# A four-layer graph network on one core: layer 3's self-interaction made during layer 2, its edge factors made for 8 tiles at a time, record gathers by fours, and five single banks for layer 0's matrices

## The chip, the core and the metric

The kernel runs on one core of a Trainium2 chip. Its metric is the device time of one execution in microseconds (us); the median of several runs is compared. Five engines work in parallel, each with its own instruction stream: TensorE (PE in the profile, with its weight loads as PEld), VectorE (DVE), ScalarE (ACT), GpSimd (POOL) and SyncE (SP), which in this kernel issues most of the plain DMA transfers. POOL issues the indirect DMAs, that is, the gathers.

## The reference, cut to what matters

8192 nodes have 32 features each. 262144 edges are sorted by their target `dst`. Each of four layers adds its result to its input and normalizes the sum over the 32 features.

```python
x = layernorm(x + segment_sum(einsum('ei,eio->eo', x[src], W0[edge_type]), dst))   # layer 0, 64 matrices of 32x32
x = layernorm(x + segment_sum(x[src] * edge_weight[:, None], dst))                 # layer 1
x = layernorm(x + segment_sum(x[src], dst))                                        # layer 2
# layer 3: s = x[:, :8], v = x[:, 8:] as (8, 3); sh = edge_attr_4, f = edge_attr_32
h = relu(f @ W1 + b1);  w = (h @ W2 + b2).reshape(e, 4, 8, 8)                      # 64 hidden, 256 weights an edge
m0 = 0.25 * (s[src]*sh0 @ w[:, 0] + C110 * (v[src] . sh1) @ w[:, 3])
m1 = 0.25 * ((s[src] @ w[:, 1]) x sh1 + v[src]*sh0 @ w[:, 2])
out = segment_sum(concat(m0, m1), dst) + SI_SCALE * concat(s @ si_w0, v @ si_w1)   # the last term: self-interaction
x = layernorm(x + out)
```

## The kernel before

The program is written as one stream per engine, in an order set by hand. `V`, `A`, `PE`, `G` and `S` are the streams of DVE, ACT, TensorE, POOL and SP. `X.mark(ins)` lets an instruction raise its engine's semaphore, `X.after(mark)` makes the next instruction of stream X wait for a mark, and `now(X)` is the last mark of X so far. A `Landing` is the same for DMAs. All buffers are cut from one arena in SBUF by `Carve`, and the eight PSUM banks (128x512 f32 each) are called by number. An edge tile is 128 edges; there are 2048 of them.

**The table stage** writes `ytab`, the product of every node with each of the 64 matrices of layer 0, in 64 tiles of 1 MB: two pairs of matmuls (L404), an eviction of each pair (L410) and one store by SP (L412). Which engine evicts is decided by `busy`: while it is true, both pairs go to ACT, afterwards the second goes to DVE. Between the tiles runs a generator, `beginnings()`, one step a tile. It counts the edges of each node and then lets POOL gather 64 sets of records (source, target and weight of the edges, in order of the nodes; 98 KB each) with `indirect` (L383). All 64 are issued in one step. `busy` becomes false at the end of the generator. It also makes `row`, the row number of each edge in `ytab`.

**Layer 0** goes over 256 groups of 8 tiles. In each group DVE makes the one-hot matrix of the targets (`one_hot`, L505) and splits the gathered rows into three bf16 parts (`parts`, L619 to L624); PE sums them by target (L657) into bank 0 or 1, four groups to a bank. POOL gathers the rows of group g+12 from `ytab`: the first half of a group waits for the sums of group g, the second half for everything that PE was given in group g. From group 8 on, PE also makes the dense matrices of layers 1 and 2 out of the records, 256 times `matrices(i)` (L555 to L581), about one in each group. These are four units of eight matmuls (L571), each into a pair of banks, 3 and 4 or 5 and 6 in turn. ACT evicts a unit with two instructions of 128x512, one (L575) for `cmat` in bf16, one (L576) for `amat` in f32, and SP stores both (L580, L581). PE waits, ahead of a unit, for L576 of the unit before the last. The generator's records first pass `slots()` at group 4. When groups enough are done, `windows` (L495) and `normalize` (L454 and the lines after) make 8 x 128 nodes of the layer's output, through bank 2.

**Layers 1 and 2** are multiplications with these matrices, read back from HBM in 32 chunks of `amat` (L730) and 16 chunks of `cmat` (L733), with two buffers. ACT copies the sums of a chunk (L739), and `turn` (L710) transposes those of the chunk before and normalizes. `normalize` of layer 2 also writes `xtab`, the table of layer 3, through SP.

**Layer 3** begins with POOL's gathers from `xtab`, by quads of four tiles; 512 quads in all. `AHEAD` is 12: the gathers of quad q+12 wait for the W2 product of quad q. Beside the first gathers PE, ACT and DVE make the self-interaction, 16 steps of transpose (L852), copy (L854), matmul (L856) and addition (L858) into `z`. `factors(s)` (L825 to L836) makes, for 32 tiles at once and with DVE, the products of gathered features and `sh`; it waits until all 32 tiles have landed. It is called once ahead of the loop and then every eighth quad, for the next 32 tiles. A step of the loop makes the hidden layer for two quads (L883) with its relu on ACT (L891), the W2 product of one quad (L907) in one of two pairs of banks, five products on DVE (L944, L947, L951 three times), the one-hot of the quad (L505), and, four quads later, the sums by target on PE (L916). `windows` and `normalize` end it.

Of the kernel before, what the change touches and what calls it, by code (L numbers as in the profile page):

```python
# [16 lines left out]
OP = mybir.AluOpType  # L17
# [7 lines left out]
D = 32  # L25
# [120 lines left out]
def raw_layers(tc, x, a, w0, w1, b1, w2, si, m, bad):  # L146
# [136 lines left out]
    def beginnings():  # L283
# [71 lines left out]
        own(V, V.e.tensor_scalar(idx2, idx, RG - 1, None, op0=OP.bitwise_and))  # L355
        im = own(V, V.e.tensor_scalar(idx, idx, RG.bit_length() - 1, None, op0=OP.arith_shift_right))

        G.after(im)
        r_ld = Landing(tc, "ld_rec")
        for k in range(64):  # L360
            begun["rec"] = r_ld.add(indirect(rg[:, k].rearrange("p s f -> p (s f)"), a["rec"], idx[:, k:k + 1]))
        yield

        own(V, V.e.tensor_tensor(pre[:, f, :], idx2, deg, op=OP.add))
        own(V, V.e.tensor_reduce(ok[:, 3:4], pre[:, f, :], AX.X, OP.max))
        V.after(src_in, row_in)
        begun["row"] = own(V, V.e.scalar_tensor_tensor(row, src, float(R), row, op0=OP.mult, op1=OP.add))
        V.e.tensor_reduce(ok[:, 0:1], rel, AX.X, OP.max)
# [171 lines left out]


    oh_used = [None, None]
    bank_free = [None, None]
    st_ld = [Landing(tc, f"st_m{k}") for k in range(2)]
# [3 lines left out]
    def matrices(i):  # L548

        b, pp, k0 = i % 2, i // 2, 16 * (i % 2)  # L550
        WB = 8
        if i % WB == 0:
            n = min(WB * 16, CB * 16 - i * 16)
            V.after(now(V))
            own(V, V.e.tensor_copy(w_ps[:, 0:n], meta_w.rearrange("p n k -> p (n k)")[:, i * 16:i * 16 + n]))  # L555
        V.after(oh_used[b])
        own(V, V.e.tensor_tensor(oh_k[:, b, :, 0, :], iota[:, None, 0:64].to_broadcast([P, 16, 64]),  # L557
                                 meta_k[:, pp, k0:k0 + 16, None].to_broadcast([P, 16, 64]), op=OP.is_equal))
        V.e.tensor_tensor(oh_l[:, b], iota[:, None, :].to_broadcast([P, 16, P]),  # L559
                          meta_l[:, pp, k0:k0 + 16, None].to_broadcast([P, 16, P]), op=OP.is_equal)  # L560
        wo = (i % WB) * 16
        vm = V.mark(V.e.tensor_tensor(oh_k[:, b, :, 1, :], oh_k[:, b, :, 0, :],
                                      w_ps[:, wo:wo + 16, None].to_broadcast([P, 16, 64]), op=OP.mult))
        PE.after(vm)
        for q in range(4):
            bk = 3 + 2 * (units[0] % 2)
            PE.after(bank_free[units[0] % 2])
            for j in range(4):
                for h in range(2):
                    hs_ = slice(64 * h, 64 * h + 64)  # L570
                    ins = PE.e.matmul(bank[:, bk + h, :].rearrange("p (c s j) -> p c s j", s=64, j=4)[:, :, :, j],  # L571
                                      oh_l[hs_, b, 4 * q + j, :], oh_k[hs_, b, 4 * q + j], start=True, stop=True)
            pm = PE.mark(ins)
            A.after(pm, st_ld[b].mark() if q == 0 and st_ld[b].n else None)
            A.e.activation(st_c[:, b, q], bank[:, bk:bk + 2, 0:256], AF.Copy)  # L575
            bank_free[units[0] % 2] = am = A.mark(A.e.activation(st_a[:, b, q], bank[:, bk:bk + 2, 256:512], AF.Copy))  # L576
            units[0] += 1
        oh_used[b] = pm
        S.after(am)
        st_ld[b].add(S.e.dma_start(amat[:, 2048 * i:2048 * (i + 1)], st_a[:, b].rearrange("p u h c -> p (u h c)")))  # L580
        st_ld[b].add(S.e.dma_start(cmat[:, 2048 * i:2048 * (i + 1)], st_c[:, b].rearrange("p u h c -> p (u h c)")))  # L581
# [5 lines left out]
    agg_free = [freed[0], freed[0]]  # L587
    acc_free = [None]
    G.after(r0, *y_done)
# [49 lines left out]
    for g in range(GG + 2):  # L639
        if g >= 2 and (g - 2) % per == per - 1:  # L640
            vm = bank_out((g - 2) // per)
            while done < NB // LC and ready(done) <= g - 1:
                pm = windows(done, bank[:, 2, 0:LC * D], (acc_free[0], vm))
                acc_free[0] = normalize(0, done, bank[:, 2, 0:LC * D], pm, x_a, x_b)
                done += 1
# [26 lines left out]
    x3 = cut(NB, 3 * D, dt=BF)  # L672
    sums = cut(2, 512)
    end = (now(PE), now(V), now(A), *stored)
    S.after(*end)
# [23 lines left out]
    pend = None  # L699
    outs = [0]  # L700

    def turn(l, c, n, am):
# [15 lines left out]
    for n, (l, c) in enumerate(seq):  # L718
# [23 lines left out]
        if pend:  # L742
            turn(*pend)
        pend = (l, c, n, am)
    turn(*pend)


    cut = Carve()
    xg = cut(4, WT, D)
    win = cut(GG, D)  # L750
    free = [now(PE), now(V), now(A)]
    taken[:] = [[None] * (WT // TP) for _ in range(4)]
# [4 lines left out]
    hs = cut(4, 512)  # L757
    si_s, sis = cut(P), cut(P)
    z = cut(NB, D)
    zx = cut(2, P)  # L760
    ef = cut(3, 2, 512)
    sh = cut(3, WT, 4)
    a0 = cut(2, WT, 16)
    vs = cut(WT, 8, 3)
    a1 = cut(WT, 8)
    vm = cut(2, WT, 3, 8)
# [6 lines left out]
    oh = cut(NO, 4, P)  # L773
    r1 = cut(24)


# [5 lines left out]
    for h in range(2):  # L782
        c_ld.add(S.e.dma_start(b1_s[64 * h:64 * h + 64], b1))
    c_ld.add(S.e.dma_start(w2_s[0:65], w2))
    zm = V.mark(V.e.memset(si_s, 0.0))
    for k in range(4):
        hm = V.mark(V.e.memset(hs[64:65, k], 1.0))  # L787
    S.after(zm)
    for q in range(4):
        c_in = c_ld.add(S.e.dma_start(si_s[q * D:(q + 1) * D, q * D:(q + 1) * D], si))  # L790

# [15 lines left out]

    AHEAD = 12
    rows = {}

    def fetch_rows(q):

        if q < NQ:
            G.after(quad.get(q - AHEAD, {}).get("w"))
            rows[q // 8] = gathers(xtab, src, q // 8, q % 8 * 4, 4)

    def factors(s):

        k, landed = rows[s]
        b = batch[s]  # L820
        b["xg"] = k
        shv = sh[:, s % 3]
        u = s % 2
        V.after(b["s"])
        sm = V.mark(V.e.tensor_scalar(shv, shv, ALPHA, None, op0=OP.mult))  # L825
        V.after(*landed, sm)
        xv = xg[:, k]
        v = xv[:, :, 8:].rearrange("p t (i m) -> p t i m", m=3)
        vmk = V.mark(V.e.tensor_tensor(vs, v, shv[:, :, None, 1:4].to_broadcast([P, WT, 8, 3]), op=OP.mult))
        V.e.tensor_tensor(a0[:, u, :, 0:8], xv[:, :, 0:8], shv[:, :, 0:1].to_broadcast([P, WT, 8]), op=OP.mult)  # L830
        V.e.tensor_tensor(vm[:, u].rearrange("p t m i -> p t i m"), v,
                          shv[:, :, None, 0:1].to_broadcast([P, WT, 8, 3]), op=OP.mult)
        V.after(vmk)
        rm = V.mark(V.e.tensor_reduce(a1, vs, AX.X, OP.add))
        V.after(rm)
        b["f"] = V.mark(V.e.tensor_scalar(a0[:, u, :, 8:16], a1, float(C110), None, op0=OP.mult))  # L836


    V.after(c_in)
    V.after(V.mark(V.e.tensor_scalar(sis, si_s, float(SI), None, op0=OP.mult)))  # L840
    fetch(0)
# [3 lines left out]
    A.after(*free)  # L845
    sv = (V.sem, V.n)
    zf = [None, None]
    for j in range(NB // 4):
        xv = x_b[:, 4 * j:4 * j + 4, :].rearrange("p d f -> p (d f)")
        u = j % 2  # L850
        PE.after(zf[u])
        tm = PE.mark(PE.e.transpose(bank[:, 3 + u, 0:P], xv, ident))  # L852
        A.after(tm)
        am = A.mark(A.e.activation(zx[:, u], bank[:, 3 + u, 0:P], AF.Copy))  # L854
        PE.after(am, sv)
        pm = PE.mark(PE.e.matmul(bank[:, 5 + u, 0:P], zx[:, u], sis, start=True, stop=True))  # L856
        V.after(pm)
        zf[u] = zm = V.mark(V.e.tensor_add(z[:, 4 * j:4 * j + 4, :].rearrange("p d f -> p (d f)"),  # L858
                                           bank[:, 5 + u, 0:P], xv))
    PE.after(*zf)  # L860
    A.after(c_in, hm)

    h_free = zm
    w_free = [zm, zm]
    agg_free = [zm, zm]
    quad = {}
# [29 lines left out]
    factors(0)  # L896
    PE.after(c_in)
    hidden(0)
    for q in range(NQ + LAG3 + 2):
# [20 lines left out]
        prev = (V.sem, V.n)  # L920
        if q % 8 == 6 and q // 8 + 1 < NS:
            s = q // 8 + 1
            factors(s)
        V.after(prev)
        if q < NQ:
            V.after(batch[q // 8]["f"])
        V.after(quad.get(q - NP, {}).get("a"))
# [10 lines left out]
        if q < NQ:  # L938
            k, wp = quad[q]["k"]
            s, u = q // 8, (q // 8) % 2  # L940
            qs = slice((q % 8) * 4, (q % 8) * 4 + 4)
            pq = p[:, q % NP]
            V.after(quad[q]["w"])
            V.e.tensor_tensor(pr[:, q % 2].rearrange("p t (o i) -> p t o i", i=8),  # L944
# [5 lines left out]
            for mm in range(3):  # L950
                V.e.tensor_tensor(pq[:, :, 128 + 64 * mm:192 + 64 * mm].rearrange("p t (o i) -> p t o i", i=8),  # L951
                                  wp[:, :, 192:256].rearrange("p t (o i) -> p t o i", i=8),
                                  vm[:, u, qs, mm, None, :].to_broadcast([P, 4, 8, 8]), op=OP.mult)
            ins = one_hot(oh[:, q % NO], 4 * q, 4)
        if ins is not None:
# [500 lines left out]
```

## Time and profile before

| | us |
|---|---|
| median of 3 runs (7660.74, 7668.28, 7670.0) | 7668.28 |
| profiled execution, its own time | 7583.78 |
| its span in the profile | 7581.8 |
| first gather from `ytab` (start of layer 0's gathers) | 271.44 |
| last gather of layer 0 starts at about | 3433.5 |
| first gather from `xtab` | 4522.57 |
| first W2 product (L907) | 4595.0 |
| last gather ends | 7500.0 |
| last sum by target (L916) ends | 7560.95 |

The profile covers one execution, on the only core; its own time is 1.1% below the median of the runs. Two groups of instructions hold nearly all of POOL's time: 2048 gathers from `ytab` (1962.0 us, 958 ns each) and 2048 from `xtab` (1967.3 us, 961 ns each). PE's largest groups are the matrices' matmuls (L571, 1566.7 us, 365 ns each), the sums of layer 3 (L916, 1420.3 us) and the W2 products (L907, 1075.3 us). In the rows of the profile a line ends with the idle time ahead of an instruction and with what released it; "remote" stands for a releaser that the profile does not name, and "issue" for time in which the engine waited for nothing that it shows.

### The profile page before, as it was taken

To read this page: it belongs to the slowest core of one execution; us is meant where nothing else is said; L and a number is where in the kernel's file an instruction comes from. 1 tells how busy PE (TensorE), PEld (TensorE's weight loads), DVE (VectorE), ACT (ScalarE), POOL (GpSimd) and SP (SyncE) were. 2 spreads that over 40 slices of the span, in tenths; PEclk is the share of its full clock that TensorE was granted. 3 is DMA by queue.
4 is the path that set the end of the run, shared out by engine and by line. 5 is a ranking of instruction groups with operands and counts; after the bars stand their busy time and mean duration, and the time that the engine had idled before them with its cause. 6 is when DMAs were issued, how large, how long until landed. Compare 5 with 4: busy or idle time off the path is not lost.

```text
span 7581.8 us, 85791 instructions
## 1 busy us (share of the span) xinstructions
PE 5254.6 (69%) x34036; PEld 3717.5 (49%) x34036; DVE 4352.7 (57%) x8312; ACT 1629.6 (21%) x2812; POOL 3996.6 (53%) x4174
## 2 busy tenths in 40 slices
PE   5326665556555665654544867889989988888998
PEld 2115555555555555553222434555555555555555
DVE  3336676677676767764000005666666667666676
ACT  3213333333333333332000001111111111111111
POOL 3466565656566666650000016666666666666663
PEclk7557677777777777777777877999998999899989
DMA  8416655556555555668999971111111111111111
GB/s 285 149 36 145 144 150 139 145 144 152 145 145 145 144 151 138 152 142 279 428 431 428 386 289 18 28 23 25 24 24 24 24 24 24 24 24 24 25 24 20
DMA packets 290731, 999.29 MB, mean 132 GB/s; under 512 B 99021, under 2 KB 175886, under 8 KB 250638
## 3 DMA queue, kind: packets, MB, share of 16 engines
q1 hardware_dynamic: 155742, 916.89, 32.2%
q0 software_dynamic: 134144, 73.67, 12.2%
q8 instruction: 269, 4.41, 0.2%
q10 hardware_dynamic: 432, 3.15, 0.1%
q14 instruction: 144, 1.18, 0.1%
HBM read 521.39 MB, written 471.99 MB: 131 GB/s over the span
## 4 chain that ended last, share of the span: by engine, by line
PE 55%; another core or an unknown queue 11%; DMA 11%; issue 9%; DVE 8%; ACT 5%; POOL 0%; SPq 0%; DVEq 0%; ACTq 0%; POOLq 0%
PE bank L571 18%; PE bank L916 14%; PE bank L907 11%; DMA f_arena<-famat 7%; PE bank L657 3%; PE bank L883 3%; DMA f_arena<-fcmat 3%; ACT f_arena L576 3%; PE bank L730 2%; PE bank L733 2%; ACT f_arena L575 2%; DVE f_arena L951 1%; DVE f_arena L505 1%; PE bank L495 1%
## 5 line engine op out<-in xcount | busy, mean ns | idle before, releaser
L383 POOL DMA_INDIRECT f_arena<-fxtab,f_src x2048 | 1967.3, 961 | 2099.2 <-DVE f_arena L787 1089.0
L383 POOL DMA_INDIRECT f_arena<-fytab,f_row x2048 | 1962.0, 958 | 1280.5 <-issue 548.2
L571 PE MATMUL bank<-f_arena 64*128 64x128 f32 x16384 | 1566.7, 365 | 963.4 <-ACT f_arena L576 682.8
L571 PEld LDWEIGHTS bank<-f_arena 64*128 64x128 f32 x16384 | 1463.3, 272 | 1100.6 <-issue 938.7
L916 PE MATMUL bank<-f_arena 128*128 128x344 f32 x4096 | 1420.3, 489 | 65.4 <-issue 63.7
L907 PE MATMUL bank<-f_arena 65*128 65x256 f32 x4096 | 1075.3, 405 | 176.2 <-issue 161.0
L916 PEld LDWEIGHTS bank<-f_arena 128*128 128x128 f32 x4096 | 842.8, 207 | 509.3 <-issue 217.5
L907 PEld LDWEIGHTS bank<-f_arena 65*128 65x128 f32 x4096 | 785.2, 198 | 559.3 <-issue 361.0
L575 ACT ACTIVATE f_arena<-bank 128x512 bf16<-128x512 f32 x1024 | 613.0, 599 | 1925.4 <-PE bank L571 816.8
L891 ACT ACTIVATE f_arena<-bank,f_arena 64x512 f32<-64x512 f32 x512 | 351.3, 686 | 2500.1 <-remote 1001.6
L557 DVE TENSOR_TENSOR f_arena<-bank,f_arena 128x1024 f32<-128x1024 f32 x256 | 313.3, 1224 | 759.8 <-PE bank L657 440.4
L505 DVE TENSOR_TENSOR f_arena<-bank,f_rel 128x512 f32<-128x512 f32 (+1 forms) x768 | 660.9, 861 | 139.9 <-ACT f_arena L537 127.7
L944 DVE TENSOR_TENSOR f_arena<-bank,f_arena 128x256 f32<-128x256 f32 x512 | 214.7, 419 | 845.0 <-PE bank L907 324.4
L576 ACT ACTIVATE f_arena<-bank 128x512 f32<-128x512 f32 x1024 | 611.7, 597 | 0.0
L559 DVE TENSOR_TENSOR f_arena<-bank,f_arena 128x2048 f32<-128x2048 f32 x256 | 586.6, 2291 | 8.8
L951 DVE TENSOR_TENSOR f_arena<-bank,f_arena 128x256 f32<-128x256 f32 x1536 | 552.0, 416 | 0.0
L730 PE MATMUL bank<-f_arena,f_x_b 128*32 128x256 f32 x4096 | 293.2, 457 | 344.9 <-DMA f_arena<-famat 344.9
L657 PE MATMUL bank<-f_arena 128*128 128x96 bf16 x2048 | 216.7, 222 | 357.7 <-issue 215.5
L730 PEld LDWEIGHTS bank<-f_arena,f_x_b 128*32 128x32 f32 x4096 | 145.1, 131 | 481.8 <-DMA f_arena<-famat 318.0
L454 DVE TENSOR_TENSOR f_lnf<-bank,f_x_b 128x256 f32<-128x256 f32 x8 | 3.4, 425 | 615.0 <-PE bank L710 615.0
L947 DVE TENSOR_TENSOR f_arena<-bank,f_arena 128x512 f32<-128x512 f32 x512 | 348.8, 681 | 0.0
L657 PEld LDWEIGHTS bank<-f_arena 128*128 128x128 bf16 x2048 | 122.0, 104 | 404.5 <-issue 260.2
(133 smaller groups left out, 3532.6 us busy)
## 6 DMA issues: line engine op xcount, KB each, us to landing
famat<-f_arena SPq DMA_DIRECT2D x256, 1024.0 KB
fcmat<-f_arena SPq DMA_DIRECT2D x256, 512.0 KB
fytab<-f_arena SPq DMA_DIRECT2D x64, 1024.0 KB
f_arena<-fytab,f_row POOLq DMA_INDIRECT x2048
f_arena<-fxtab,f_src POOLq DMA_INDIRECT x2048
f_arena<-laid_ea SPq DMA_DIRECT2D x64, 512.0 KB
f_arena<-laid_ea SPq DMA_DIRECT2D x64, 64.0 KB
f_arena<-laid_xT ACTq DMA_DIRECT2D x1, 1024.0 KB, 8.9
```

Source lines behind the costliest of these rows:

```text
L383: return G.e.indirect_dma_start(out=dest, out_offset=None, in_=table, in_offset=bass.IndirectOffsetOnAxis(ap=ix, axis=0))
L505: return V.e.tensor_tensor(o, iota[:, None, :].to_broadcast([P, n, P]), rel[:, t:t + n, None].to_broadcast([P, n, P]), op=OP.is_equal)
L559: V.e.tensor_tensor(oh_l[:, b], iota[:, None, :].to_broadcast([P, 16, P]), meta_l[:, pp, k0:k0 + 16, None].to_broadcast([P, 16, P]), op=OP ...
L571: ins = PE.e.matmul(bank[:, bk + h, :].rearrange("p (c s j) -> p c s j", s=64, j=4)[:, :, :, j], oh_l[hs_, b, 4 * q + j, :], oh_k[hs_, b, ...
L575: A.e.activation(st_c[:, b, q], bank[:, bk:bk + 2, 0:256], AF.Copy)
L576: bank_free[units[0] % 2] = am = A.mark(A.e.activation(st_a[:, b, q], bank[:, bk:bk + 2, 256:512], AF.Copy))
L657: ins = PE.e.matmul(bank[:, bk, 3 * c * D:3 * (c + 1) * D], oh[:, h, t, :], xp[:, g % 4, t].rearrange("p c f -> p (c f)"), start=(t == 0), ...
L730: ins = PE.e.matmul(bank[q * D:(q + 1) * D, b, 0:256].rearrange("p (u h j) -> p u h j", h=2, j=4), x_b[:, s, :], mv[:, s], start=(s < 4), ...
L891: quad[q + h] = dict(h=A.mark(A.e.activation(hs[0:64, (q + h) % 4], bank[64 * h:64 * h + 64, 2, :], AF.Relu, bias=b1_s[64 * h:64 * h + 64])))
L907: ins = PE.e.matmul(wp[:, t, :], hs[0:65, q % 4, t * P:(t + 1) * P], w2_s[0:65], start=True, stop=True)
L916: ins = PE.e.matmul(bank[:, g % 2, 0:MW], oh[:, c % NO, t, :], p[:, c % NP, t, :], start=(c % 2 == 0 and t == 0), stop=(c % 2 == 1 and t = ...
L951: V.e.tensor_tensor(pq[:, :, 128 + 64 * mm:192 + 64 * mm].rearrange("p t (o i) -> p t o i", i=8), wp[:, :, 192:256].rearrange("p t (o i) - ...
```

## The change

The records are gathered four at a time. After each four, the generator gives back control for two tiles of the table (for one, from the 48th on), and POOL waits for what PE has been given by then. So the generator, and with it `busy`, ends near the 60th tile. `row` is made earlier.

The matrices of layer 0 use a ring of five single banks, 2 to 6. Each bank is evicted by two ACT instructions of 128x256, and is given free by itself. PE still waits once ahead of a unit, for both of its banks. `windows` and `normalize` of layer 0 use the bank of the sums that have just been taken out.

The self-interaction is made by `self_part(j)`. Fourteen of its 16 parts go into layer 2, two after every second chunk from chunk 3 on; the last two follow the last `turn`. Its memset and its loads come at the start of layer 1, and its buffers stay in the arena under those of layer 3.

In layer 3 `AHEAD` is 8. `factors(r)` works on 8 tiles, every second quad, one step ahead of their use. The one-hot of a quad stands ahead of the wait for W2.

```diff
+        V.after(src_in, row_in)
+        begun["row"] = own(V, V.e.scalar_tensor_tensor(row, src, float(R), row, op0=OP.mult, op1=OP.add))
         for k in range(64):
+            if k % 4 == 0 and k:
+                for _ in range(2 if k < 48 else 1):
+                    yield
+                G.after(now(PE))
             begun["rec"] = r_ld.add(indirect(rg[:, k].rearrange("p s f -> p (s f)"), a["rec"], idx[:, k:k + 1]))
...
-    bank_free = [None, None]
+    bank_free = {k: (acc_free[0] if k == 2 else None) for k in range(2, 7)}
...
-            bk = 3 + 2 * (units[0] % 2)
-            PE.after(bank_free[units[0] % 2])
+            bk = [2 + (2 * units[0] + h) % 5 for h in range(2)]
+            PE.after(*(bank_free[b5] for b5 in bk))
...
-            A.e.activation(st_c[:, b, q], bank[:, bk:bk + 2, 0:256], AF.Copy)
-            bank_free[units[0] % 2] = am = A.mark(A.e.activation(st_a[:, b, q], bank[:, bk:bk + 2, 256:512], AF.Copy))
+            for h in range(2):
+                A.e.activation(st_c[:, b, q, h], bank[:, bk[h], 0:256], AF.Copy)
+                bank_free[bk[h]] = am = A.mark(A.e.activation(st_a[:, b, q, h], bank[:, bk[h], 256:512], AF.Copy))
...
-                pm = windows(done, bank[:, 2, 0:LC * D], (acc_free[0], vm))
-                acc_free[0] = normalize(0, done, bank[:, 2, 0:LC * D], pm, x_a, x_b)
+                acc = bank[:, (g - 2) // per % 2, 0:LC * D]
+                agg_free[(g - 2) // per % 2] = vm = normalize(0, done, acc, windows(done, acc, (vm,)), x_a, x_b)
...
+    def self_part(j):
+        xv = x_b[:, 4 * j:4 * j + 4, :].rearrange("p d f -> p (d f)")
+        u = j % 2
+        if j == 0:
+            V.after(si_in)
+            own_part[0] = V.mark(V.e.tensor_scalar(sis, si_s, float(SI), None, op0=OP.mult))
+        PE.after(ln_last[0], zf[u], own_part[0])
+        tm = PE.mark(PE.e.transpose(bank[:, 4 + u, 0:P], xv, ident))
+        A.after(tm)
+        PE.after(A.mark(A.e.activation(zx[:, u], bank[:, 4 + u, 0:P], AF.Copy)), zf[1 - u])
+        V.after(PE.mark(PE.e.matmul(bank[:, 6, 0:P], zx[:, u], sis, start=True, stop=True)))
+        zf[u] = V.mark(V.e.tensor_add(z[:, 4 * j:4 * j + 4, :].rearrange("p d f -> p (d f)"), bank[:, 6, 0:P], xv))
...
         if pend:
             turn(*pend)
+        if l == 2 and c >= 3 and c % 2 == 1:
+            self_part(c - 3)
+            self_part(c - 2)
         pend = (l, c, n, am)
     turn(*pend)
+    free = [now(PE), now(V), now(A)]
+    self_part(NB // 4 - 2)
+    self_part(NB // 4 - 1)
...
-    AHEAD = 12
+    AHEAD = 8
...
             G.after(quad.get(q - AHEAD, {}).get("w"))
-            rows[q // 8] = gathers(xtab, src, q // 8, q % 8 * 4, 4)
+            rows[q // 2] = gathers(xtab, src, q // 8, q % 8 * 4, 4)
...
-        V.after(*landed, sm)
-        xv = xg[:, k]
+        V.after(landed[-1], factor.get(r - 1))
+        xv = xg[:, k, ts]
...
-        b["f"] = V.mark(V.e.tensor_scalar(a0[:, u, :, 8:16], a1, float(C110), None, op0=OP.mult))
+        factor[r] = V.mark(V.e.tensor_scalar(a0[:, u, ts, 8:16], a1, float(C110), None, op0=OP.mult))
...
-        if q % 8 == 6 and q // 8 + 1 < NS:
-            s = q // 8 + 1
-            factors(s)
+        if q % 2 == 0 and q + 2 < NQ:
+            factors(q // 2 + 1)
...
+            one_hot(oh[:, q % NO], 4 * q, 4)
             V.after(quad[q]["w"])
...
-            ins = one_hot(oh[:, q % NO], 4 * q, 4)
```

## The prediction

> **What bounds the kernel now.** I read the page's rows first (which engine is full), then stretches of each stage, then single rows at the seams. TensorE is busy 69% of the span and no engine is full throughout, so the answer differs by stage. The columns of the stretches are us, busy time (x instructions) of PE, weight load, DVE, ACT and POOL, then the granted clock, DMA share, GB/s.
>
> ```profile
> span 7581.8 us, 85791 instructions
> PE 5254.6 (69%) x34036; PEld 3717.5 (49%) x34036; DVE 4352.7 (57%) x8312; ACT 1629.6 (21%) x2812; POOL 3996.6 (53%) x4174
> 140.00:160.00 20.00, 4.15 (x8) 1.01 (x8) 1.23 (x1) 1.02 (x1) 15.12 (x17) 0.50 0.43 131
> 220.00:240.00 20.00, 18.74 (x62) 6.79 (x56) 8.57 (x7) 7.30 (x8) 0.00 (x0) 0.50 1.03 380
> 1000.00:2000.00 1000.00, 593.15 (x6130) 530.59 (x6126) 687.05 (x867) 362.59 (x686) 614.51 (x650) 0.73 0.58 145
> 4550.00:4600.00 50.00, 13.66 (x34) 7.52 (x35) 6.73 (x15) 4.14 (x9) 25.49 (x27) 0.50 0.07 9
> 5000.00:6000.00 1000.00, 901.98 (x3145) 577.57 (x3146) 689.14 (x1789) 121.36 (x180) 654.70 (x687) 0.91 0.13 24
> 7502.00:7560.00 58.00, 57.69 (x211) 37.74 (x211) 47.29 (x127) 6.86 (x10) 0.00 (x0) 0.96 0.00 1
> ```
>
> The table stage runs at 380 GB/s at 220, at the DMA engines' limit (share 1.03), but only at 131 GB/s at 140, while POOL issues the 64 record gathers without a pause: 8 matmuls in 20 us. Layer 3 needs 5.75 to 5.80 us a quad (four tiles) while POOL gathers, and 4.7 in its last 58 us, when the gathers are over and PE is full (57.69 of 58.00). The next rows show why. One gather is 0.95 us plus 0.30 before it: 1.25 us. Columns: start, duration, engine, line, operation, and in brackets the idle time before it with its releaser.
>
> ```profile
> 2032.72 0.95 POOL L383 DMA_INDIRECT f_arena<-fytab,f_row  x1 [0.30 <-issue]
> 2035.36 0.60 ACT L575 ACTIVATE f_arena<-bank 128x512 bf16<-128x512 f32 x1 [4.65 <-PE bank L657]
> 2035.76 0.95 POOL L383 DMA_INDIRECT f_arena<-fytab,f_row  x1 [2.09 <-PE bank L657]
> 2044.51 0.95 POOL L383 DMA_INDIRECT f_arena<-fytab,f_row  x1 [0.30 <-issue]
> 2047.48 0.95 POOL L383 DMA_INDIRECT f_arena<-fytab,f_row  x1 [2.03 <-remote]
> 4522.57 0.95 POOL L383 DMA_INDIRECT f_arena<-fxtab,f_src  x1 [1089.02 <-DVE f_arena L787]
> 4566.81 0.29 DVE L858 TENSOR_TENSOR f_arena<-bank,f_x_b 128x128 f32<-128x128 f32 x1 [8.11 <-remote]
> 4575.21 0.29 DVE L858 TENSOR_TENSOR f_arena<-bank,f_x_b 128x128 f32<-128x128 f32 x1 [8.11 <-remote]
> 4599.10 0.95 POOL L383 DMA_INDIRECT f_arena<-fxtab,f_src  x1 [16.80 <-PE bank L907]
> 5481.72 0.95 POOL L383 DMA_INDIRECT f_arena<-fxtab,f_src  x1 [3.14 <-PE bank L907]
> 5504.77 0.94 POOL L383 DMA_INDIRECT f_arena<-fxtab,f_src  x1 [3.35 <-PE bank L907]
> ```
>
> While POOL issues gathers back to back, whoever waits for PE is told late: ACT and DVE wait 4.65 and 8.11 us for matmuls that take half a microsecond, and are released about 1.65 us after POOL's last gather has ended (2033.67 to 2035.36). So POOL's uninterrupted runs, not PE's work, set the pace. In layer 0 this locks: 8 gathers (10.0 us) and a pause of 2.0, 11.76 us for each of 256 groups. In layer 3 POOL runs 12 or 16 gathers (three or four quads, 16.8 or 23.0 us with the pause).
>
> **The change part by part.** The profiled execution took 7583.8 us (span 7581.8), 1.1% less than the runs' median of 7668.28. I sum against the former and carry the difference over to the median.
>
> *Records by fours.* The 64 gathers end at 191.0 and the table's last store is waited for until 271.44 (POOL's first gather from the table, after 80.4 idle). From 112.7, where the gathers begin to hold the tiles, 34 of the 64 remain. Undisturbed tiles of 1 MB come every 2.4 to 2.75 us, so 34 x 2.75 = 93.5 plus 6.3 MB of records at 380 GB/s, 16: ready at 222. From the other side: if each group of four holds up the tiles for its 5.0 us plus the 2.0 pause, 16 x 7 = 112 us and some remaining tiles, about 250. POOL's new waits hold only the generator's own gathers; nothing else is queued on it there. I take -40, nearer to the first because a tile's two matmul pairs get through in the early part of a burst (range -15 to -55). The tiles' second halves now go to ACT for about 26 more tiles (DVE's copies 30 to 4); a tile takes 2 x 1.0 on ACT, under the 2.75 of its store: 0. The row numbers, made earlier, wait for loads that have long landed: 0. The next thing late is the store itself.
>
> *Five banks in layer 0.* Nothing is removed from PE; each of 1024 units gets four evictions of 128x256 instead of two of 128x512. The rows give 0.599 and 0.597 for these, and 0.412 for the nearest 128x256 copy (layer 1's sums, L739): 1.65 against 1.20, +0.45 us a unit, +461 us of ACT. [...] Both lie in ACT's idle time, which is 64% of this stage; it costs something only where PE waits for ACT. PE did wait 682.8 us for L576, but mostly inside the lock: what came late there was PE's report, and unit u still waits for the evictions of u-2 by ring. About 12 groups with two matrices, and the last 11 groups after the last gather at 3433.5, do run on PE and ACT; 0.4 to 0.7 us each: -8 in all. Between the bounds (a longer ACT chain at the end of each group, +0.1 x 256, and a shorter one) I hold -30 to +30. Windows move from bank 2 to the sums' own bank, so eight normalizations keep that bank some 5 us; the other bank takes the next four groups (47 us): 0.
>
> *Self-interaction during layer 2.* 16 steps leave the start of layer 3. Undisturbed a step takes 1.38 us. Fourteen go, two at a time (2.8 us), behind the turn of every second chunk, where PE then waits 2.0 to 8.6 us for the next chunk's DMA (21.9 us a chunk, PE needs 16.8 + 1.0). SP issues nothing new there; its four small loads go to the start of layer 1, behind one memset, and the first two chunks are already queued. Cover gone, this is 7 x 2.8 = 20. Only the pair at the last chunk stands before the last turn, with no DMA left to hide it: +2.8. The last two parts follow the last turn.
>
> *Lead 8 and factors by 8 tiles.* Before: POOL starts at 4522.6, gathers 12 quads (60.0), then idles 16.8, because factors for 32 tiles need 8 quads landed, the self steps crawl at up to 8.1 each, and W2 starts only at 4595. Then 500 quads x 5.80, and 61 for the last (POOL ends 7500.0, last L916 7560.95): 7561. After: 4525.4 + 8 quads x 5.0 = 40, during which the first factors (two quads landed) and the first hidden layers are already made, no long idle, 504 x 5.80, and a tail of 8 quads instead of 12, 61 - 4 x 4.7 = 42: 7531. That is -30, the last chunk's +2.8 included (range -15 to -45; less if POOL first idles once for W2).
> Factors cost DVE more. Rows: L829 128x768 0.960 us, L830 128x256 0.420, which gives a slope of 1.055 ns an element and 0.15 fixed; a set over 8 tiles is 0.35 + 0.22 + 0.49 + 0.345 + 0.19 = 1.6, four sets 6.4 against 4.1: +2.3 x 64 = +146 us of DVE. [...] by the trace DVE is 69% busy here and waits 845 us for W before L944, so it is hidden: 0. That cover shrinks to 26%. POOL waits on W2 of the quad eight back, DVE needs quads q+2 and q+3 at quad q: five to six quads in hand, as against three at worst before. The one-hot of a quad (L505, 0.86 us) now stands ahead of the wait for W2, so in such a wait 0.86 of products come earlier; where reports set the pace this too is worth 0. SP's loads and POOL's queue have the same order as before, in smaller pieces. The pace stays 5.80, within 0.08 a quad: ±40.
>
> Sum: -40 - 8 - 30 = -78, say -80: 7504 for the profiled execution, and 7588 for the median.
>
> **The rivals.**
> R1, five banks break layer 0's lock. If ACT's finer releases let PE's reports and POOL's next eight gathers overlap, the pause of 2.0 goes down to 0.3: 256 x 1.75 = 450. For: 682.8 us of PE waits name L576. Against: POOL also waits for the group's own matmul, and the pause equals the 1.65 us by which reports lag. Half of it gives 7588 - 200 = 7390.
> R2, the slower side: the lead of 8. If POOL, having only eight quads of credit, stops after every quad, the cycle is that of the 26 one-quad bursts that the trace has, 7.0 us against 5.75: +1.25 each. It decides from 80 / 1.25 = 64 extra such quads of 512 on; if a quarter of all (128) go this way, +160 - 80: 7750. DVE's shrunken cover would push the same way. Against: bursts end after 12 or 16 gathers, below either lead, because W2's report fails to come, not for want of credit.
> R3, the records' fours each cost their full 7 us and layer 3's start keeps an idle of ten: -15 - 15: 7635.
> R4, the chain absorbs it: the time saved in front is lost again to a different burst pattern in layers 0 and 3 (±0.06 us a quad is 30 us), so that nothing measurable remains: 7668.
>
> **How the numbers follow.** Main case 0.65 (7550 to 7625 by the sums of the bounds), R1 0.07, R2 0.12, R3 0.10, R4 0.06. No change is what this kernel's measurement can't tell, 0.2% or 15 us. Faster: main, R1 and R3, 0.82; same 0.06; slower 0.12. Leaving out R1 and R2, the range is 7520 to 7655.
>
> **What would show it.** Record gathers in fours from 110 to some 205, and the first gather from the table at about 225 instead of 271.4; evictions of 0.41; layer 0 still at 11.76 us a group with pauses of 2.0; L907 first at about 4535 instead of 4595, and no idle of 16.8 us on POOL after its first quads; bursts still of 12 and 16 gathers; 42 us from POOL's last gather to the last L916. Wrong would be: layer 0's group under 11.5 us (R1), over 90 bursts of four gathers in layer 3 (R2), DVE waiting less than 300 us for W in layer 3, or layer 2 longer by over 10 us.

## The result and the profile after

The changed kernel takes 7594.94 us (median; 7590.36 to 7595.86) beside 7664.51 for the kernel before: a ratio of 0.9911, 95% interval 0.9896 to 0.9925, which is 57 to 80 us less; the medians differ by 70. (Here and below "us less" and "us more" without a range are differences of medians; a ratio is taken over all runs and can differ a little from the quotient of the medians.) In a second set of runs the ratio was 0.9909 (0.9893 to 0.9924). The forecast was 7588, 80 us less.

The profiled execution that the prediction worked from was itself 1% quicker than the kernel usually is. A second profile of the kernel before (`before2` below, span 7635.0) is the better partner for after. The stages, in us, from the first and last instructions of each:

| | before, as shown | before2 | after | after2 |
|---|---|---|---|---|
| first gather from `ytab` | 271.4 | 271.7 | 231.0 | 229.4 |
| layer 0's gathers, first to last | 3162 | 3200 | 3223 | 3212 |
| layers 1 and 2: from there to POOL's first gather of layer 3 | 1089 | 1072 | 1077 | 1074 |
| layer 3, from there to the end | 3059 | 3091 | 3057 | 3053 |
| span | 7581.8 | 7635.0 | 7588.5 | 7568.8 |

From before2 to after2 that is -42 + 12 + 2 - 38 = -66. Of the forecast's three terms, the records by fours and layers 2 and 3 brought about what was forecast; layer 0, where the five banks are, got longer.

The same stretches of after as were shown of before (us, then busy time and instructions of PE, weight load, DVE, ACT, POOL; granted clock, DMA share, GB/s):

```profile
span 7588.5 us, 89476 instructions
PE 5411.7 (71%) x34036; PEld 3845.9 (51%) x34036; DVE 4372.1 (58%) x9246; ACT 1780.4 (23%) x4886; POOL 3972.9 (52%) x4174
140.00:160.00 20.00, 17.99 (x66) 6.61 (x62) 0.00 (x0) 14.65 (x17) 13.26 (x15) 0.67 1.03 383
1000.00:2000.00 1000.00, 633.56 (x5982) 559.45 (x5984) 672.19 (x851) 395.73 (x1336) 606.21 (x642) 0.66 0.54 142
4550.00:4600.00 50.00, 21.27 (x56) 13.59 (x56) 17.28 (x49) 2.74 (x4) 31.87 (x34) 0.56 0.08 12
5000.00:6000.00 1000.00, 908.39 (x3128) 585.20 (x3127) 700.92 (x2095) 119.35 (x176) 648.93 (x685) 0.91 0.12 25
```

At 140 us the table is now written at 383 GB/s, where it stood at 131 before, with nearly as many gathers beside it (15 for 17). For layer 0 the right partner is again before2:

```profile
1000.00:2000.00 1000.00, 603.84 (x6058) 536.51 (x6060) 679.90 (x858) 358.05 (x678) 606.52 (x642) 0.72 0.52 144
```

As many gathers get through in these 1000 us as in after (642 in both; the shown profile of before had 650), PE is busier in after (634 us for 604) and its clock lower (0.66 for 0.72). Rows of the timeline at the seams:

```profile
154.94 0.95 POOL L387 DMA_INDIRECT f_arena<-laid_rec,f_arena  x1 [1.86 <-PE bank L408]
172.38 0.95 POOL L387 DMA_INDIRECT f_arena<-laid_rec,f_arena  x1 [2.70 <-remote]
204.82 0.94 POOL L387 DMA_INDIRECT f_arena<-laid_rec,f_arena  x1 [0.30 <-issue]
230.99 0.95 POOL L387 DMA_INDIRECT f_arena<-fytab,f_row  x1 [25.22 <-DMA fytab<-f_arena]
2044.77 0.95 POOL L387 DMA_INDIRECT f_arena<-fytab,f_row  x1 [0.30 <-issue]
2047.50 0.39 ACT L581 ACTIVATE f_arena<-bank 128x256 bf16<-128x256 f32 x1 [3.14 <-remote]
2047.89 0.95 POOL L387 DMA_INDIRECT f_arena<-fytab,f_row  x1 [2.17 <-remote]
4531.24 0.95 POOL L387 DMA_INDIRECT f_arena<-fxtab,f_src  x1 [1077.09 <-PE bank L730]
4541.45 7.20 PE L923 MATMUL bank<-f_arena 65*128 65x256 f32 x16
4586.38 0.42 DVE L960 TENSOR_TENSOR f_arena<-bank,f_arena 128x256 f32<-128x256 f32 x1 [21.38 <-remote]
4586.61 0.95 POOL L387 DMA_INDIRECT f_arena<-fxtab,f_src  x1 [5.30 <-remote]
4640.18 0.95 POOL L387 DMA_INDIRECT f_arena<-fxtab,f_src  x1 [2.73 <-remote]
4657.69 0.94 POOL L387 DMA_INDIRECT f_arena<-fxtab,f_src  x1 [2.81 <-PE bank L923]
```

The first two rows are ends of pauses between record gathers, and the third is the last record gather. The table is ready at 231. Layer 0 is still locked: the last gather of a run starts at 2044.77, ACT is released 1.78 us after its end, POOL after a pause of 2.17. Over all of layer 0 POOL pauses 244 times (for more than half a us) in before2 and in after, for 689 and 712 us in all. In layer 3 the first W2 product (L923, formerly L907) comes 10.2 us after POOL's first gather, and the idle behind the first quads is 5.3 us; the last two rows are ends of pauses between runs of twelve gathers. The pace of layer 3 did not change. From the end of the first idle to the last gather, before2 needs (7555.1 - 4621.8) / 500 = 5.87 us a quad, after (7529.8 - 4586.6) / 502 = 5.86.

### The profile page after: what moved, and what is told of

It is laid out like the page before. It is cut to its first block, busy times and chain, and to the rows that moved or that the text cites. A ratio compares the mean times of both kernels' runs of the same rounds, so it can differ in the third digit from the quotient of the medians.

```text
span 7588.5 us, 89476 instructions
## 1 busy us (share of the span) xinstructions
PE 5411.7 (71%) x34036; PEld 3845.9 (51%) x34036; DVE 4372.1 (58%) x9246; ACT 1780.4 (23%) x4886; POOL 3972.9 (52%) x4174
## 4 chain that ended last, share of the span: by engine, by line
PE 43%; another core or an unknown queue 17%; DVE 15%; DMA 10%; ACT 9%; issue 5%; POOL 1%; SPq 0%; DVEq 0%; ACTq 0%; POOLq 0%
PE bank L576 14%; PE bank L932 11%; PE bank L923 10%; DMA f_arena<-famat 6%; ACT f_arena L582 4%; ACT f_arena L581 4%; DVE f_arena L967 3%; DMA f_arena<-fcmat 3%; PE bank L899 2%; PE bank L761 2%; DVE f_arena L963 2%; DVE f_arena L509 2%; PE bank L764 2%; PE bank L408 1%
## 5 line engine op out<-in xcount | busy, mean ns | idle before, releaser
L387 POOL DMA_INDIRECT f_arena<-fxtab,f_src x2048 | 1942.9, 949 | 2132.7 <-PE bank L730 1077.1
L576 PE MATMUL bank<-f_arena 64*128 64x128 f32 x16384 | 1626.3, 374 | 894.9 <-ACT f_arena L582 567.9
L576 PEld LDWEIGHTS bank<-f_arena 64*128 64x128 f32 x16384 | 1519.4, 280 | 989.5 <-ACT f_arena L582 477.4
L923 PE MATMUL bank<-f_arena 65*128 65x256 f32 x4096 | 1107.2, 417 | 207.6 <-DVE f_arena L967 194.8
L581 ACT ACTIVATE f_arena<-bank 128x256 bf16<-128x256 f32 x2048 | 817.5, 399 | 1847.6 <-remote 1024.0
L923 PEld LDWEIGHTS bank<-f_arena 65*128 65x128 f32 x4096 | 808.2, 204 | 603.6 <-DVE f_arena L967 297.2
L907 ACT ACTIVATE f_arena<-bank,f_arena 64x512 f32<-64x512 f32 x512 | 351.0, 686 | 2564.8 <-remote 1156.7
L582 ACT ACTIVATE f_arena<-bank 128x256 f32<-128x256 f32 x2048 | 828.6, 405 | 0.0
L960 DVE TENSOR_TENSOR f_arena<-bank,f_arena 128x256 f32<-128x256 f32 x512 | 214.1, 418 | 836.6 <-remote 368.6
L662 PE MATMUL bank<-f_arena 128*128 128x96 bf16 x2048 | 273.4, 261 | 364.8 <-issue 230.5
L662 PEld LDWEIGHTS bank<-f_arena 128*128 128x128 bf16 x2048 | 150.7, 120 | 484.4 <-issue 361.5
```

The costliest lines, as they stand in the source:

```text
L387: return G.e.indirect_dma_start(out=dest, out_offset=None, in_=table, in_offset=bass.IndirectOffsetOnAxis(ap=ix, axis=0))
L576: ins = PE.e.matmul(bank[:, bk[h], :].rearrange("p (c s j) -> p c s j", s=64, j=4)[:, :, :, j], oh_l[hs_, b, 4 * q + j, :], oh_k[hs_, b, 4 ...
L581: A.e.activation(st_c[:, b, q, h], bank[:, bk[h], 0:256], AF.Copy)
L582: bank_free[bk[h]] = am = A.mark(A.e.activation(st_a[:, b, q, h], bank[:, bk[h], 256:512], AF.Copy))
L662: ins = PE.e.matmul(bank[:, bk, 3 * c * D:3 * (c + 1) * D], oh[:, h, t, :], xp[:, g % 4, t].rearrange("p c f -> p (c f)"), start=(t == 0), ...
L923: ins = PE.e.matmul(wp[:, t, :], hs[0:65, q % 4, t * P:(t + 1) * P], w2_s[0:65], start=True, stop=True)
```

## The experiments

Lines of the kernels below are numbered as in the kernel before, shifted by one or two where an edit adds lines. The first set ran beside a kernel before of 7642.97 us.

**The kernel before once more (before2).**

> The kernel before, unchanged, once more, for a second profile of it. Theory A (the shown profile of before, 1.1% under its median, is the odd one): this run takes about 7660, with layer 0's gathers lasting about 3220 us instead of 3162 and layer 3 about 3080 instead of 3059. Theory B (the five banks cost layer 0 some 60 us): layer 0's gathers last 3162 here too, and the 80 us that are missing lie elsewhere.

It took 7636.94 (one execution), with layer 0's gathers lasting 3200 us and layer 3 3091. So theory A holds for layer 3 and for most of layer 0's difference (3162 to 3200); from 3200 to 3223 is left for theory B.

**Records by fours alone (p_rec).** The edit is the first part of the diff.

> The kernel before with only the records gathered by fours. My theory: 40 us less than before (first gather from the table at 231 instead of 271), nothing later changed: about 7625. Rival: the 40 us are given back in layer 0, whose pace is set by POOL's cycle: within 15 us of 7664.

7603.1, ratio 0.9942 (0.9929 to 0.9956): 40 us less. Its trace has the table's rate at 140 us and the seam moved as in after, while layer 0's gathers last 3200 us as in before2; nothing is given back. So the edit is shown to bring the 40 us. How it brings them is not shown: it makes POOL wait between fours, and it also keeps `busy` true for longer, so that ACT alone evicts (no DVE instruction in this stretch, where before alternates between ACT and DVE). The waits are short. In after, POOL issues twelve record gathers without a stop from 154.94 on, to the pause that ends at 172.38, and from 156 to 172 the table still goes out at 394 GB/s:

```profile
156.00:172.00 16.00, 11.49 (x42) 4.30 (x44) 0.00 (x0) 9.43 (x10) 10.43 (x11) 0.71 1.04 394
```

Pauses or evictions by ACT alone: this was not run apart. The rows of p_rec itself:

```profile
140.00:160.00 20.00, 15.67 (x62) 5.26 (x58) 0.00 (x0) 13.54 (x15) 13.34 (x15) 0.74 1.04 383
229.09 0.95 POOL L387 DMA_INDIRECT f_arena<-fytab,f_row  x1 [25.18 <-DMA fytab<-f_arena]
```

**Five banks alone (p_banks).** The edit is the diff's part on `bank_free`, `bk`, the evictions and the windows.

> The kernel before with only the five single banks in layer 0. My theory: POOL's cycle of 8 gathers and a pause of 2.0 us stays, so 8 us less at most: 7656 within 15. Rival 1: the longer chain of evictions lengthens each group by 0.2 us: about 7715. Rival 2: the lock is loosened: under 7600.

7658.63, ratio 1.0017 (1.0010 to 1.0025): 16 us more, against a forecast of 8 less: the direction of rival 1, at a third of its size.

**Layers 2 and 3 alone (p_l3).** The edit is the rest of the diff.

> The kernel before with only the changes of layers 2 and 3 (self-interaction made in layer 2, lead of 8, factors by 8 tiles). My theory: 30 us less from layer 3's start and tail: about 7634, with layer 3 taking 3030 from POOL's first gather. Rival: the pace of layer 3 is slower by 0.05 us a quad, which gives the 30 us back: about 7664.

7610.14, ratio 0.9955 (0.9941 to 0.9969): 33 us less; 3050 us from POOL's first gather to the end, where before2 has 3091. The three parts sum to -40 + 16 - 33 = -57, at the edge of the interval of the whole (57 to 80).

The next four kernels ran where the kernel before takes 6476.85 us, 15% less. Nothing in the program differs, but the chip does: on record the set above ran on chip 0, this one on chip 12. What is different in it is not known.

**Windows in the sums' bank alone (p_win).**

```diff
-                pm = windows(done, bank[:, 2, 0:LC * D], (acc_free[0], vm))
-                acc_free[0] = normalize(0, done, bank[:, 2, 0:LC * D], pm, x_a, x_b)
+                acc = bank[:, (g - 2) // per % 2, 0:LC * D]
+                agg_free[(g - 2) // per % 2] = vm = normalize(0, done, acc, windows(done, acc, (vm,)), x_a, x_b)
```

> The kernel before with one edit: windows and normalize of layer 0 work in the bank of the sums that were just taken out, not in bank 2. The five banks by themselves took 16 us more than before. Theory W (the shared bank costs this): plus 15 here. Theories C and A (below): within 6 us of before.

6477.56, ratio 1.0001 (0.9992 to 1.0009). This says nothing about the 16 us, because the lock that they arose in is absent here. Two stretches and two of POOL's waits (us in total, times, longest) of this kernel, with none of the pauses:

```profile
140.00:160.00 20.00, 13.71 (x48) 4.59 (x48) 7.00 (x6) 5.89 (x7) 15.13 (x17) 0.50 1.04 395
1000.00:2000.00 1000.00, 627.19 (x7634) 580.81 (x7634) 855.00 (x1086) 450.78 (x854) 755.89 (x802) 0.81 0.67 181
POOL f_arena L383 <- DMA fytab<-f_arena: 33.2, 1, 33.2
POOL f_arena L383 <- PE bank L907: 23.6, 40, 2.6
```

POOL issues the same 64 record gathers without a pause, 17 of them in this stretch, and the table is written beside them at 395 GB/s; in the profile of before that the prediction shows, the same 17 left 131 GB/s. In layer 0 there are 802 gathers in 1000 us, one each 1.25 us, and no wait for L657 among POOL's longer ones (449.0 us in before2). PE's reports, that is, its semaphores as the waiting engine sees them, come on time here although POOL never stops. Take the units whose end ACT waited for: from the last matmul of a unit, as the profile models its end, to ACT's first eviction it takes 0.05 us here in the median and under 0.2 in 99 of 100, but in before2 1.1 us in the median and over 6.1 in one of ten.

**Narrow evictions alone (p_split).**

```diff
-            A.e.activation(st_c[:, b, q], bank[:, bk:bk + 2, 0:256], AF.Copy)
-            bank_free[units[0] % 2] = am = A.mark(A.e.activation(st_a[:, b, q], bank[:, bk:bk + 2, 256:512], AF.Copy))
+            for h in range(2):
+                A.e.activation(st_c[:, b, q, h], bank[:, bk + h, 0:256], AF.Copy)
+                bank_free[units[0] % 2] = am = A.mark(A.e.activation(st_a[:, b, q, h], bank[:, bk + h, 256:512], AF.Copy))
```

> The kernel before with one edit: each unit of layer 0's matrices, still in two pairs of banks, is evicted by four instructions of 128x256 instead of two of 128x512. Theory A (the longer chain on ACT, 1.60 us for 1.20, makes the five banks dearer): plus 15 or more. Theory C (finer releases let PE work in shorter, denser runs, so that its clock is granted less often): the release comes later here, not earlier, so the granted clock of layer 0 stays at 0.72 or above and the time within 6 us of before, or some 5 more for the later release.

6475.13, ratio 0.9998 (0.9989 to 1.0006): nothing, where POOL alone sets layer 0's pace.

**Five banks with wide evictions (p_ring2).**

```diff
+            if bk[1] == bk[0] + 1:
+                A.e.activation(st_c[:, b, q], bank[:, bk[0]:bk[0] + 2, 0:256], AF.Copy)
+                am = A.mark(A.e.activation(st_a[:, b, q], bank[:, bk[0]:bk[0] + 2, 256:512], AF.Copy))
+                bank_free[bk[0]] = bank_free[bk[1]] = am
+            else:
...
```

> The five banks, but with wide evictions (two of 128x512, both banks given free by the second) where a unit's banks lie side by side, which is four times in five; windows in the sums' bank as there. Theory C: releases come as late as before, so the clock of layer 0 returns to about 0.72 and most of the 16 us go: plus 3. Theory A: plus 3 too. Theory W: plus 15, as p_win.

6477.01, ratio 1.0000 (0.9992 to 1.0008). Inconclusive for the same reason.

**The change without the five banks (no_banks).** Windows are back in bank 2 too.

> The changed kernel without the five banks (records by fours, self-interaction in layer 2, lead 8 and factors by 8). If the parts add up: 40 + 33 = 73 us less than before, ratio 0.9905, and 16 less than the changed kernel. Rival: the parts don't add, the clock takes it back: ratio 0.992 or more.

6434.68, ratio 0.9936 (0.9922 to 0.9949): 42 us less. All of it is layer 3: POOL's first gather comes at 3814.2 (3814.9 in p_win), the first gather from `ytab` at 226.1 (225.0), and layer 3 takes 2618 us for 2663. The tail after the last gather shrinks from 56 to 24 us. The records by fours are worth nothing where reports are not late.

The third set, on chip 3, ran again beside a kernel before of 7636.58 us.

**Self-interaction in layer 2 alone (p_self).** Lead 12, factors by 32 tiles, one-hot where it was.

> The kernel before with only the self-interaction moved into layer 2; lead 12 and factors by 32 tiles as before. My theory: the idle of 16.8 us behind POOL's first twelve quads goes, the tail stays at 60 us, and the last chunk of layer 2 takes 2.8 more: 14 to 17 us less than before, about half of what all the changes of layers 2 and 3 bring. Rival: the first factors still wait for eight quads and hold the start, so that nearly nothing comes of it, under 5 us.

7624.93, ratio 0.9985 (0.9978 to 0.9992): 12 us less, between the two forecasts but nearer to mine. The idle behind the first quads shrinks but does not go, for DVE's first factors still wait until eight quads have landed. Rows of POOL, of before2, p_self (with DVE's first factor) and p_l3 in turn:

```profile
4621.80 0.95 POOL L383 DMA_INDIRECT f_arena<-fxtab,f_src  x1 [17.68 <-PE bank L907]
```
```profile
4590.98 0.96 DVE L855 TENSOR_TENSOR f_arena<-f_arena 128x768 f32<-128x768 f32 x1 [36.13 <-DMA f_arena<-fxtab,f_src]
4640.07 0.94 POOL L383 DMA_INDIRECT f_arena<-fxtab,f_src  x1 [10.71 <-remote]
```
```profile
4611.95 0.95 POOL L383 DMA_INDIRECT f_arena<-fxtab,f_src  x1 [6.12 <-remote]
```

So of the 33 us some 12 are the self-interaction's, and some 21 are left for lead and factors, which were only run together: mostly the tail after the last gather, 59 us in before2, 60 in p_self and 40 in p_l3.

**Narrow evictions alone, once more (p_split2).**

> Once more the kernel before with evictions of 128x256 in two pairs of banks, since the run before fell on a chip where POOL never pauses in layer 0. Where POOL does pause there (before takes about 7650): theory A (longer ACT chain) plus 15; theories C (finer releases, lower clock) and W (shared bank) within 6 of before, and the granted clock of layer 0 at 0.72 or above. Where POOL does not pause (before takes about 6480): 0 again.

7717.94, ratio 1.0105 (1.0090 to 1.0121): 81 us more, in theory A's direction but five times as large as it said. The clock is 0.69, where theory C expected 0.72 or above. The stretch of layer 0 in before2, p_split2 and p_banks in turn, each with POOL's waits for the matrices' matmuls and for the sums:

```profile
700.00:3300.00 2600.00, 1555.06 (x15685) 1379.75 (x15682) 1759.96 (x2229) 926.51 (x1753) 1571.99 (x1663) 0.72 0.52 143
POOL f_arena L383 <- PE bank L657: 449.0, 187, 20.7
POOL f_arena L383 <- PE bank L571: 114.7, 23, 10.0
```
```profile
700.00:3300.00 2600.00, 1567.80 (x15324) 1393.06 (x15326) 1721.20 (x2176) 1016.74 (x3421) 1530.33 (x1622) 0.69 0.52 140
POOL f_arena L383 <- PE bank L571: 396.2, 114, 11.1
POOL f_arena L383 <- PE bank L658: 305.5, 115, 20.8
```
```profile
700.00:3300.00 2600.00, 1639.74 (x15553) 1449.54 (x15550) 1741.77 (x2206) 1029.65 (x3472) 1557.09 (x1651) 0.66 0.55 143
POOL f_arena L383 <- PE bank L658: 436.7, 174, 20.7
POOL f_arena L383 <- PE bank L572: 207.5, 42, 9.7
```

Before, POOL mostly waits for the sums (L657; L658 in the other two). With narrow evictions alone it waits 396 us for the matrices (L571), which now come last more often: ACT's work is inside the lock's circle. In p_banks this falls to 207.5. Layer 0's 244 pauses, sorted by where they stand, say the same. In us in all:

| | before2 | p_split2 | p_banks |
|---|---|---|---|
| 13 pauses of over 8 us | 135 | 138 | 128 |
| 21 pauses at the seven normalizations between gathers | 89 | 110 | 108 |
| the other 210 | 465 | 524 | 479 |
| of these, how many last over 2.5 us | 0 | 65 | 2 |

What narrow evictions cost in ordinary groups, 59 us, the ring takes down to 14. What it leaves is mostly at the normalizations, +20 us. These are as long in p_split2, whose windows stay in bank 2, so moving the windows is not needed for them. The five profiles with wide evictions (before, before2, p_rec, p_self, p_l3) have 80 to 95 us there. ACT's rows show how long a unit takes, of before2 and then p_split2; the first three rows are a wide unit and the start of the next, the last five a narrow unit and the start of the next:

```profile
2033.00 0.60 ACT L575 ACTIVATE f_arena<-bank 128x512 bf16<-128x512 f32 x1 [4.69 <-remote]
2033.49 0.59 ACT L576 ACTIVATE f_arena<-bank 128x512 f32<-128x512 f32 x1
2033.97 0.61 ACT L575 ACTIVATE f_arena<-bank 128x512 bf16<-128x512 f32 x1
```
```profile
2032.54 0.38 ACT L576 ACTIVATE f_arena<-bank 128x256 bf16<-128x256 f32 x1 [3.89 <-remote]
2032.82 0.38 ACT L577 ACTIVATE f_arena<-bank 128x256 f32<-128x256 f32 x1
2033.08 0.39 ACT L576 ACTIVATE f_arena<-bank 128x256 bf16<-128x256 f32 x1
2033.34 0.41 ACT L577 ACTIVATE f_arena<-bank 128x256 f32<-128x256 f32 x1
2033.61 0.42 ACT L576 ACTIVATE f_arena<-bank 128x256 bf16<-128x256 f32 x1
```

A wide unit occupies ACT for 0.97 us from start to start, a narrow one for 1.07. That is 0.10 us a unit, 102 us over 1024 units, beside 81 us in the time. That the first makes all of the second is not shown: PE's clock fell as well, and the matmuls of the matrices (L571) kept it busy for 1631 us instead of 1578. These 54 us may be a part of the 81; the runs do not separate them.

**The changed kernel once more (after2).**

> The changed kernel once more. Where POOL pauses in layer 0 (before about 7650): ratio 0.991 to 0.9925, as the parts add up to (40 - 16 + 33 = 57) or as first measured (70). Where it does not (before about 6480): the five banks and the fours of records are worth nothing, the ratio is that of the kernel without the five banks there, 0.9936, within 0.001.

7568.94, ratio 0.9909 (0.9893 to 0.9924), 68 us less, as at first. Both times the whole gains some 11 to 13 us more than the parts' sum of 57, within the intervals; why, if it is real, is open.

**The change without the five banks, once more (no_banks2).**

> The changed kernel without the five banks, once more, for a chip on which POOL pauses in layer 0. Where it does (before about 7640): ratio 0.989 if the five banks cost the changed kernel what they cost alone (16 us), that is better than both kernels; 0.991 if they cost nothing in its company. Where it does not (before about 6480): 0.9936 again.

It ran on chip 4, where the kernel before takes 6476.46, and gave 0.9937 (0.9923 to 0.9950) again. So the version that should beat both kernels where POOL pauses was not measured there. From the parts it would be some 73 us below the kernel before, an estimate.

## Why the prediction was right, and where it was not

The time (7595 for a forecast of 7588) and the range held. Of the sum's three terms two held, and one had the wrong sign: the parts alone gave -40, +16 and -33, where -40, -8 and -30 were forecast. That the total came within 10 us owes something to luck, since the 24 us that the banks missed were in part made up by a whole that gains more than its parts.

*Records by fours.* Forecast -40; alone -40, with the table ready at 231 for a forecast of 222 to 250. That tiles get through beside the gathers is what p_rec's 383 GB/s shows; that the waits between the fours are what lets them through is not shown, since evictions moved from DVE to ACT with the same edit.

*Layers 2 and 3.* Forecast -30, measured -33. "No long idle" was 5.3 us instead of none, since a report is late there as well (DVE waits 21.38 us ahead of the product at 4586.38). The tail came to 38 us (forecast 42). The pace stayed: DVE's added work was hidden (its waits ahead of L944, now L960, still sum to 836 us, 869 in before2). That the factors' tiles have 64 to 192 elements now costs nothing that shows in the pace (5.86 us a quad for 5.87). Between pauses of over half a us, after has 148 runs of twelve gathers and 46 of four, before2 126 and 44, so R2, the lead of 8 as a brake, did not happen. Runs of sixteen, 63 in the first profile of before and 19 in before2, are gone. R1 did not happen either: the 244 pauses of layer 0 stayed, their median 2.27 us for 2.22.

*Five banks.* Forecast -8, measured +16. The step that failed is to put ACT's added time "in ACT's idle time, which is 64% of this stage; it costs something only where PE waits for ACT", with the 682.8 us of such waits set aside as lying inside the lock. ACT idles for 64% of this stage and still stands in the chain that closes its cycles: POOL's next eight gathers need PE's matrices, and these need ACT's releases. Narrow evictions alone cost 81 us, and POOL's waits for the matrices went from 114.7 to 396.2 us. "Unit u still waits for the evictions of u-2" was wrong too: with five single banks it waits only for the first half of them (its first bank was last used by u-3). The earlier release should be what gives back 81 - 16 = 65 us, an estimate across two sets of runs, in which the moved windows and the clock take part. The small gain that was forecast for the groups with two matrices is seen (POOL's pauses of over 8 us sum to 128 us in p_banks and 135 in before2), and is lost among the others. That ACT's time inside the lock is the cause of the 81 us rests on one edit and on where the pauses grew (65 of the ordinary ones over 2.5 us, for none); the share of the clock in it is open. Where the 16 us stand is seen, mostly at the normalizations; why narrow evictions lengthen those is not known.

*Sizes read from rows.* ACT's extra was put at +461 us from durations. Its rows do sum to 817.5 + 828.6 = 1646 us for 1225 before, but they overlap: in 2600 us of layer 0 ACT is occupied for 1030 us in p_banks instead of 927, about the 0.10 a unit above. (A single 128x256 eviction took 0.40 us, 817.5 / 2048, where the row that the prediction took has 0.412.) The same holds for the factors on DVE: 424 us of rows after, 277 before, yet DVE's occupied time between 4620 and 7500 goes from 1957 to 2008 only.

*The profiled execution.* It was forecast at 7504 and took 7590.36, since the shown profile of before was 1% under its runs and that of after is not. Carrying the difference to the median was the right choice; trusting the shown profile's layer 0 (3162 us) was not.

*The claim beneath it all,* that PE's reports come late while POOL issues gathers, holds in the runs at 7640 and not in those at 6477, with the same program (from a unit's last matmul to ACT 1.1 us in the median of before2, 0.05 in p_win). Nor does it hold throughout in the profile of before: from 4529.64 to 4536.54 six additions of the self-interaction (L858) follow each other 1.38 us apart while POOL gathers, and only later ones 8.4 apart.

```profile
4531.02 0.29 DVE L858 TENSOR_TENSOR f_arena<-bank,f_x_b 128x128 f32<-128x128 f32 x1 [1.09 <-PE bank L856]
4531.32 0.95 POOL L383 DMA_INDIRECT f_arena<-fxtab,f_src  x1 [0.30 <-issue]
4532.40 0.29 DVE L858 TENSOR_TENSOR f_arena<-bank,f_x_b 128x128 f32<-128x128 f32 x1 [1.09 <-PE bank L856]
4532.58 0.94 POOL L383 DMA_INDIRECT f_arena<-fxtab,f_src  x1 [0.30 <-issue]
4533.78 0.29 DVE L858 TENSOR_TENSOR f_arena<-bank,f_x_b 128x128 f32<-128x128 f32 x1 [1.09 <-issue]
```

At 6477 the change without the five banks is worth 0.6%, all of it from layer 3; the whole change was not run there.

*Slips in the working.* The pace of 11.76 us is not that of each of 256 groups: 3162 / 256 is 12.35, since 13 pauses last over 8 us, and most of those at the normalizations 3 to 6. The matmuls of a unit, for which ACT waits 4.65 us, take 1.2 to 2.1 us, not half a microsecond. The 23 groups at 0.4 to 0.7 us give -9 to -16, not -8; half of R1's 450 leads to 7363, not 7390; R3's two terms lead to 7638, not 7635. None of these moves the argument.

## What to carry to other kernels

Ask of each engine not only how idle it is but whether the stage's slowest circle passes through it: here an edit to an engine that idled 64% cost 81 us. Where a long series of gathers holds up the other engines, try to issue it in pieces between their work: here that edit brought the table from 131 GB/s (before, 17 gathers in 20 us) to 383 (p_rec, 15 gathers), and which side of it did so is open. Take an instruction's cost in a train from start to start, not from its duration (0.49 us for 0.60 in the rows of before2), and profile the kernel before twice before resting a sum on it (7581.8 and 7635.0 here).

## What the runs showed of the hardware

The same kernel took about 7640 us on chips 0 and 3 and 6477 on chips 12 and 4, steadily within a set. Most of the difference goes with POOL's pauses: in layer 0 before2 has 244 of them, 689 us in all, and in layer 3 some 190, 480 us in all; in p_win there are none in layer 0 and seven, 13 us in all, in layer 3.

TensorE's granted clock stands in the profile of before at half and at full in turn, 366 stretches of each, and in that of after 387 of each; all but the last stretch of either last 3.41 us or a multiple of it. In layer 0 of before2 (from 700 to 3300 us) each 3.41 us, with the share of it that PE was busy, stands against the clock of the next 3.41 us as follows. After half clock, full clock came in all of 169 cases with PE busy for 90% or more, in 31 of 47 between 80% and 90%, and in 2 of 215 below that. After full clock, it came again in all of 85 cases above 60%, in 43 of 70 between 50% and 60%, and in one of 177 below. The same count in before gives 176 of 176, 27 of 37 and none of 200, and 107 of 111, 37 of 89 and one of 149. These are counts of two profiles and no more than that.

In p_banks the clock of this stretch is lower (0.66, 0.72 in before2): only 41 of 251 stretches of 3.41 us at full clock are half busy or more (155 of 332 in before2; 52 of 258 in after, 200 of 349 in before), full clock is granted for 33% of the time instead of 43%, and about the same number of matmuls keeps PE busy longer (1640 us for 1555). I took this for the effect of earlier releases, after which PE would finish its matmuls sooner and then idle; that was my estimate, which no run shows. p_split2 (clock 0.69) speaks against it as the only reason: its releases come later, and full clock falls too, to 38% of the time, with 86 of 287 such stretches half busy. How much of the 16 us, or of the 81, the lower clock makes was not separated.
